# Attention with kept exponentials on one core: the exchange between partition groups goes through a buffer in DRAM, and SyncE's transfers stand in program order

## The chip, the cores and the metric

The kernel runs on one core of a Trainium2 chip (8 cores); the other cores are idle. The metric is the time of one execution on the device in microseconds. A core has TensorE (PE; PEld is its weight load), VectorE (DVE), ScalarE (ACT), GpSimd (POOL) and SyncE (SP, which only issues transfers). POOL, ACT and SP can each put transfers on a queue of their own; the 16 DMA engines of the core work on all of these queues.

## The reference

```python
# x: 8 x 512 x 512, cond: 8 x 512, all float32; 16 heads of 32
Q, K, V   = heads(x @ Wq.T + bq), heads(x @ Wk.T + bk), heads(x @ Wv.T + bv)
tQ, tK    = heads(tokens @ Wq.T + bq), heads(tokens @ Wk.T + bk)   # tokens = cond[:, None, :]
scores    = (Q + tQ) @ (K + tK).T / sqrt(32)
attn      = softmax(scores, axis=-1)
out       = x + (attn @ V, heads joined)
```

## The kernel before, in words

The work is cut into 32 steps `t`, one for each batch and each group of four heads (8 batches of 4 groups). The scores of a step are made twice. First they come row by row (128 queries on the partitions, 512 keys along the free axis): PE makes them (L640), DVE takes the negative row maximum (`nmax`, L592 and L649), and ACT takes the exponentials and their row sums (L700). Of these exponentials half the queries (two blocks of 128) are *kept* for steps 1 to 29 (`KEPT`). For the other half of the queries the scores are made a second time in transposed form (keys on the partitions, L784, after L771 has put the row maxima in), and ACT takes their exponentials (L798). `weighted` (L839) then multiplies exponentials by V, first the half made again, then the kept half; `send` turns the result (L911), scales it (L912), adds the residual `xr` (L913) and stores it (L916).

The kept exponentials have queries on the partitions and must have keys there before L839 can use them. That takes two things. `turn_kept` (L659), four DVE instructions a step, transposes every 32x32 block in place. Then the blocks must change places between the four *partition groups* of 32 partitions: the part at group `a`, place `g` changes with the part at group `g`, place `a`. A part is 32 partitions of 1024 floats, 128 KB; there are six such pairs. `swap_kept(t, move)` does this inside SBUF in three moves: each pair's first part goes aside, the second takes its place, and the part put aside goes to the second's place. That is 18 transfers of 128 KB a step. Some are issued by SP (`nc.sync`) and some by POOL (`nc.gpsimd`): move 2 always by POOL, and of move 0 either none or the last four, so that POOL issues 6 or 10 of them a step.

The loop is `thirds(t, made)` for t = 1 to 28, with three parts `i` = 0, 1, 2. At its start stands `weighted(t - 1)`. Within it the exponentials of step t + 1 are kept and turned, and at its end moves 0 and 1 of step t + 1 are issued; move 2 of step t is issued in part 1. So the parts of step t + 1 set out at the end of `thirds(t)`, and L839 wants them in `thirds(t + 2)`. Beside this work PE makes the projections of the next batch (L461), a third of a set in each part.

The other transfers of a step are SP's: `load_block` (L172) brings an input block `x` in four transfers of 64 KB, `load_residual` (L190) `xr` in four, `send` (L916) stores the output in four, and `turn_max` (L726) is one transposing transfer from `split` to `maxT`, which L771 needs a step later. `split_max` (L714 to L717, on POOL) makes what it reads.

`manual_schedule` names the engines whose instructions stay in the order in which the code is written. Here these are PE, ACT, DVE and POOL; SP is not among them, and the order of its transfers is made by the framework.

Of the kernel before, what the change touches and what calls it, by code (L numbers as in the profile page):

```python
# [9 lines left out]
F32 = mybir.dt.float32  # L10
# [7 lines left out]
def kernel(  # L18
# [38 lines left out]
    nc = tc.nc  # L57
    P = 128
    B, S, D = x.shape
# [3 lines left out]
    HG = P // HD  # L63
# [14 lines left out]
    op = ctx.enter_context(tc.tile_pool(name="op", bufs=2))  # L78
    ring = ctx.enter_context(tc.tile_pool(name="ring", bufs=1, space=bass.MemoryType.PSUM))

    psum = ring.tile([P, 8, 512], F32, tag="psum", name="psum")


# [32 lines left out]
    def banks(i, n=1):  # L116

        row = row_of[0] or [at_end[j] for j in TURNS[turn[0]]]
        j = row[i]
        if n == 1:  # L120
            return psum[:, j, :]
        k = row[i + 1]
        return psum[:, j : k + 1 : k - j, :]
# [103 lines left out]
    def load_w(n, w, queue, cs=range(NC)):  # L227
        wv = w.rearrange("(c p) d -> p c d", p=P)
        for c in cs:
# [7 lines left out]
                mybir.EngineType.Activation,  # L237
                mybir.EngineType.DVE,
                mybir.EngineType.Pool,
            }  # L240
        )
    )
# [415 lines left out]
        e = kept[t][:, :, n // NP, pr, :].rearrange("p g h s -> p g (h s)")  # L658
        nc.vector.transpose(e, e)  # L659

    APART = [(a, g) for a in range(HG) for g in range(a + 1, HG)]
    between = store[:, 16:18]

    def swap_kept(t, move, some=range(6)):

        later = 6 if t % 4 == 1 else 2

        def part(a, g):
            return kept[t][a * BL : (a + 1) * BL, g].rearrange("p c h s -> p (c h s)")

        for n in some:
            a, g = APART[n]
            at = (n + 2) % HG * BL
            aside = (store[:, 6:8] if t == KEPT[-1] else between)[at : at + BL, n // HG]
            aside = aside.rearrange("p i s -> p (i s)")
            to, of = [(aside, part(a, g)), (part(a, g), part(g, a)), (part(g, a), aside)][move]
            if t < KEPT[-1]:
                here = move == 2 or move == 0 and n >= later
            else:
                here = move > 0 and n >= 3  # L680
            (nc.gpsimd if here else nc.sync).dma_start(to, of)  # L681

    def denominators(t, qc, w=HG, js=range(HG)):

        if t >= T - 2:
            return
        keep = t in KEPT and qc < KQ
        if keep and t not in kept:
            kept[t] = room(t)
        for j in js:  # L690
            of = to = banks((w or 0) + j)
            if w is None and j == 0:
                of = to = spare
# [193 lines left out]
    def weighted(t, pt, pd, between):  # L887

        apart = masked(t)
        if t in KEPT:
            of = (0, 2, 1, 3)
            for half in (1, 0):
                for kc in of:
                    times_v_half(t, kc, half, pt, of)
                if half == (t + 1 not in KEPT):
                    spread_sums(apart, pd)
        else:
            for kc in range(NS):  # L900
                times_v(t, kc, pt)
                if kc == (NS - 1 if t + 1 in KEPT else 0):
                    spread_sums(apart, pd)
        rec = reciprocals(t, pd)
        between()
        send(t, pt, rec)
# [195 lines left out]
    turn_kept(1, 3)  # L1102
    combine_x(1, 1, nc.gpsimd)
    aparts[0] = masked(0)
    for move in range(2):
        swap_kept(1, move)

    MADE = [
        (n, u, product)
# [45 lines left out]
    def thirds(t, made):  # L1155

        b, r = divmod(t, G)
        of = (t - 1) // G + 1
        begin(0, HG)
        turn_more(t, 0, 0)  # L1160
        row_max_aside(t + 1, 1)
        max_aside(t + 1, 1)
        row_max(t + 1, 2, False, HG)
        turn_more(t, 0, 1)
        denominators(t + 1, 1, None, (1, 2, 3, 0))
        denominators(t + 1, 2, HG)
        weighted(t - 1, banks(0), banks(1), nothing)
        turn_more(t, 0, 2)
        load_blocks(1)
        one_item(of, *next(made), (2, 3), ignore, nothing)  # L1170
        released(0, 1, 4, 5, 7, 6, 2, 3)
        for i in (1, 2):
            begin(HG)
            rows = (t + 1, 3) if i == 1 else (t + 2, 0)
            if i == 1:
                joined(t, i - 1, rows)
                turn_more(t, i, 0)
                row_max(*rows, False, HG, False)
            else:
                exponentials_of_rest(t, i - 1)  # L1180
                turn_more(t, i, 0)
                row_max(*rows, False, HG)
            turn_more(t, i, 1)
            if i == 1:
                first = range(6 if t + 1 < KEPT[-1] else 3)
                swap_kept(t, 2, first)
                split_max(t + 1)
                turn_max(t + 1)
                swap_kept(t, 2, range(len(first), 6))
            dens = lambda js=range(HG): denominators(*rows, HG, js)  # L1190
            n, u, kind = next(made)
            if kind == "first":
                products(of, n, u, kind, False, dens, nothing, None)
                turn_more(t, i, 2)
            elif n == "v":
                small = nothing
                if t + 1 not in KEPT:
                    small = lambda: transpose_max(t + 1, banks(2), nc.scalar.copy)
                other_shared(of, n, u, dens, (0, 3), small, lambda: turn_more(t, i, 2))
                released(1, 2, 4, 5, 6, 7, 0, 3)  # L1200
            else:
                products(of, n, u, kind, False, dens, nothing, False)
                turn_more(t, i, 2)
            if i == 1:
                aparts[t] = masked(t)
            if (t + 1, i) == (KEPT[-1], 1):
                swap_kept(t + 1, 0)
            if i == 2:
                if r == 0:
                    combine_x(b + 1, 1, nc.gpsimd)  # L1210
                load_residual(t + 1)
            else:
                if t > 1:
                    bias_residual(t)
                if r == 0:
                    combine_x(b + 1, 0, nc.gpsimd)
            if i == 2 and t + 1 < KEPT[-1]:
                for move in range(2):
                    swap_kept(t + 1, move)

    def other_shared(b, n, u, dens, at, small, more):

# [115 lines left out]
        row_max_of(t + 1, 2, 1, banks(HG + 2, 2))  # L1338
    row_max_of(t + 1, 2, 0, late[0][:, :2, :])
    bias_residual(t)  # L1340
    swap_kept(t, 1)
    apart = masked(t - 1)
    aparts[t] = masked(t)
    load_residual(t + 2)
    bias_residual(t + 2)
    swap_kept(t, 2)
    load_residual(t + 1)
    halves_of(t - 1, banks(0), (1,))
    row_of[0] = [*second[:2], *first[2:], *first]
# [150 lines left out]
```

## Time and profile before

| | |
|---|---|
| median of 3 runs | 650.57 us (649.7 to 651.48) |
| the profiled execution | 650.74 us, span of the core 648.9 us |
| PE, DVE, ACT, POOL busy | 642.6, 600.7, 533.6, 409.6 us |
| granted clock of TensorE | 1.0 |
| transfers between places in SBUF | 264 issued by SP, 258 by POOL, 128 KB each |
| queue of SP (q1) | 65.54 MB, packets took 53.3% of 16 engines' span |
| queue of POOL (q0) | 33.83 MB, packets took 19.2% of 16 engines' span |

The time of a run is a little longer than the span, 650.74 against 648.9 us for the same execution. A queue's share is the time that its packets took, added over the 16 DMA engines and divided by 16 spans: 53.3% of 648.9 us are 346 us in which all 16 engines would be busy with that queue.

### The profile page before, as it was taken

The page shows a single profiled execution, that of the slowest core. Times are in us where ns is not written, and L with a number is a line of the kernel's source. Part 1 is how long each engine was busy: PE and PEld are TensorE (multiplying, and loading weights), DVE is VectorE, ACT ScalarE, POOL GpSimd, SP SyncE. Part 2 cuts the span into 40 slices and gives each one's busy share as a digit, 9 for nine tenths or more (in the row PEclk, how much of TensorE's full clock was granted, in tenths as well). Part 3 has the DMA queues.
Part 4 walks back from the last instruction along what each step waited for, and adds up shares of the span by engine and source line. Part 5 has one row for each costly group of instructions (what it writes and reads, how often), then busy time and mean ns, then how long its engine had stood idle before and what let it go on. Part 6 is the DMA issues. An engine that isn't in the chain of part 4 may idle for free. (4 is left out here: it accounts for less than half of the span.)

```text
span 648.9 us, 24878 instructions
## 1 busy us (share of the span) xinstructions
PE 642.6 (99%) x9856; PEld 358.5 (55%) x9856; DVE 600.7 (93%) x845; ACT 533.6 (82%) x1364; POOL 409.6 (63%) x651
## 2 busy tenths in 40 slices
PE   9999999999999999999999999999999999999997
PEld 8445555556555555555555555555655555555541
DVE  3799999999999999999999999999999999999887
ACT  2479888889888889888888988898988888888564
POOL 3642555767666785668566585766767677675650
PEclk9999999999999999999999999999999999999999
DMA  7634588788779788878788887897877777777821
GB/s 187 106 48 68 121 183 175 158 180 178 155 172 181 156 190 181 190 155 172 173 184 172 171 170 152 177 198 158 180 152 180 176 162 153 165 177 161 201 37 33
DMA packets 248456, 102.01 MB, mean 157 GB/s; under 512 B 229962, under 2 KB 230474, under 8 KB 248340
## 3 DMA queue, kind: packets, MB, share of 16 engines
q1 hardware_dynamic: 234196, 65.54, 53.3%
q0 software_dynamic: 12384, 33.83, 19.2%
q8 instruction: 78, 1.28, 0.8%
q10 hardware_dynamic: 1760, 1.05, 0.6%
q14 instruction: 38, 0.31, 0.2%
HBM read 19.75 MB, written 8.39 MB: 43 GB/s over the span
## 5 line engine op out<-in xcount | busy, mean ns | idle before, releaser
L592 DVE TENSOR_REDUCE nmax<-psum 128x1 f32<-128x512 f32 x279 | 177.8, 676 | 9.9 <-PE psum L640 5.1
L681 POOL DMA_DIRECT2D store<-store x258 | 128.9, 502 | 77.3 <-DMA store<-store 51.9
L700 ACT ACTIVATE psum<-psum,nmax 128x512 f32<-128x512 f32 x248 | 165.1, 678 | 3.6 <-DVE nmax L592 3.0
L640 PE MATMUL psum<-kT,qT 32*128 32x512 f32 x1024 | 161.8, 612 | 0.0
L700 ACT ACTIVATE store<-psum,nmax 128x512 f32<-128x512 f32 x204 | 139.5, 700 | 24.7 <-DVE nmax L592 24.5
L798 ACT ACTIVATE store<-psum 128x512 f32<-128x512 f32 x232 | 119.8, 603 | 33.4 <-PE psum L784 33.4
L659 DVE STREAM_TRANSPOSE store<-store 128x1024 f32<-128x1024 f32 x116 | 138.9, 1217 | 0.0
L649 DVE TENSOR_REDUCE nmax<-psum 128x2 f32<-128x1024 f32 x98 | 118.9, 1213 | 0.0
L839 PE MATMUL psum<-store,v 128*32 128x256 f32 x1856 | 107.1, 381 | 0.6 <-issue 0.6
L839 PEld LDWEIGHTS psum<-store,v 128*32 128x32 f32 x1856 | 57.2, 110 | 57.9 <-ACT wT_q L631 21.2
L784 PE MATMUL psum<-qT,kT 32*128 32x256 f32 x928 | 83.8, 373 | 0.0
L640 PEld LDWEIGHTS psum<-kT,qT 32*128 32x128 f32 x1024 | 61.3, 183 | 35.5 <-issue 17.8
L912 POOL TENSOR_TENSOR res<-res,recs 128x512 f32<-128x512 f32 x30 | 31.4, 1045 | 75.4 <-DVE res L911 75.4
L784 PEld LDWEIGHTS psum<-qT,kT 32*128 32x128 f32 x928 | 60.8, 184 | 5.7 <-issue 0.3
L700 ACT ACTIVATION_READ_ACCUMULATOR psum<-psum,nmax 128x1 f32 x248 | 55.1, 222 | 0.0
L461 PE MATMUL psum<-wc_v,xc 128*32 128x256 f32 x768 | 47.7, 379 | 0.0
L203 POOL TENSOR_TENSOR xr<-xr,bvs 128x512 f32<-128x512 f32 x30 | 38.3, 1276 | 11.1 <-DMA x<-in_x_dram 11.1
L461 PE MATMUL psum<-xc,wc_q 128*32 128x256 f32 x720 | 44.8, 379 | 0.0
L461 PE MATMUL psum<-xc,wc_k 128*32 128x256 f32 x720 | 44.5, 379 | 0.0
L700 ACT ACTIVATION_READ_ACCUMULATOR store<-psum,nmax 128x1 f32 x204 | 44.4, 218 | 0.0
L913 POOL TENSOR_TENSOR res<-res,xr 128x512 f32<-128x512 f32 x30 | 38.3, 1276 | 2.4
L461 PE MATMUL psum<-xT,wT_k 128*32 128x256 f32 x480 | 34.5, 382 | 0.0
(191 smaller groups left out, 975.4 us busy)
## 6 DMA issues: line engine op xcount, KB each, us to landing
store<-store SPq DMA_DIRECT2D x264, 128.0 KB, 2.9
store<-store POOLq DMA_DIRECT2D x258, 128.0 KB, 3.8
out_dram<-res SPq DMA_DIRECT2D x122, 64.0 KB, 3.7
xr<-in_x_dram SPq DMA_DIRECT2D x120, 64.0 KB, 3.4
x<-in_x_dram SPq DMA_DIRECT2D x112, 64.0 KB, 3.5
w_q<-in_L_cond_Wq_dram SPq DMA_DIRECT2D x4, 256.0 KB, 4.5
w_v<-in_L_cond_Wv_dram SPq DMA_DIRECT2D x16, 64.0 KB, 2.5
w_k<-in_L_cond_Wk_dram SPq DMA_DIRECT2D x16, 48.0 KB, 2.8
```

Of the source, the lines that this page charges most:

```text
L203: nc.gpsimd.tensor_tensor(xr[t], xr[t], bias, ALU.add)
L461: nc.tensor.matmul(pt[r], still[:, r], moving, start=(kc == kcs[0]), stop=(kc == kcs[-1]))
L592: nc.vector.tensor_reduce(nmax[t][:, qc, j : j + 1, 0], pt, AX.X, ALU.max, negate=True)
L640: nc.tensor.matmul(pt, qkT["q", t][r, qc * P : (qc + 1) * P], qkT["k", t][r, :], start=True, stop=True,)
L649: nc.vector.tensor_reduce(nmax[t][:, qc, pr * 2 : pr * 2 + 2, 0], pt, AX.X, ALU.max, negate=True)
L659: nc.vector.transpose(e, e)
L681: (nc.gpsimd if here else nc.sync).dma_start(to, of)
L700: nc.scalar.activation(to, of, AF.Exp, bias=nmax[t][:, qc, j, :], accum_out=sums[t][:, qc, j, :],)
L784: nc.tensor.matmul(banks(j)[:, i * HS : (i + 1) * HS], qkT["k", t][r, kc * P : (kc + 1) * P], qkT["q", t][r, KQ * P :], start=False, stop= ...
L798: nc.scalar.activation(e[:, j], banks(j), AF.Exp)
L839: nc.tensor.matmul(pt[j * HD : (j + 1) * HD, half * HS : (half + 1) * HS], vs[b % 2][:, kc, (g * HG + j) * HD : (g * HG + j + 1) * HD], e, ...
L913: nc.gpsimd.tensor_tensor(y, y, xr.pop(t), ALU.add)
```

## The change

The six pairs no longer change places inside SBUF. A buffer in DRAM (pool `outside`, two buffers, `outer[t]`) takes all parts that have to move, in six writes of one to three parts each (`write_kept`), and six reads (`read_kept`) bring them back to their new places. Together that is 12 parts written and 12 read. The parts on the diagonal stay where they are. All twelve transfers are issued by SP; POOL issues none.

SP joins the engines with a written order. With this the places of the calls are set by hand: the writes of step t + 1 stand at the end of `thirds(t)`, behind them the loads of `x` and of `xr`; the reads of step t stand in part 0 of `thirds(t)`, ahead of `weighted(t - 1)` and so ahead of its stores. The two chunks of SBUF that were used to put parts aside stay reserved.

```diff
+    outside = ctx.enter_context(
+        tc.tile_pool(name="outside", bufs=2, space=bass.MemoryType.DRAM)
+    )
...
                 mybir.EngineType.Pool,
+                mybir.EngineType.SP,
...
-    APART = [(a, g) for a in range(HG) for g in range(a + 1, HG)]
-    between = store[:, 16:18]
-    def swap_kept(t, move, some=range(6)):
...
-            (nc.gpsimd if here else nc.sync).dma_start(to, of)
+    OTHERS = [(0, 1, 4), (1, 0, 1), (1, 2, 4), (2, 0, 2), (2, 3, 4), (3, 0, 3)]
+    def write_kept(t):
+        outer[t] = outside.tile([HG, BL, HG, NP * 2 * S // 2], F32, tag="kept", name=f"outer_{t}")
+        of = kept[t].rearrange("p g c h s -> p g (c h s)")
+        for a, lo, hi in OTHERS:
+            nc.sync.dma_start(outer[t][a, :, lo:hi], of[a * BL : (a + 1) * BL, lo:hi])
+    def read_kept(t):
+        to = kept[t].rearrange("p g c h s -> p g (c h s)")
+        for g, lo, hi in OTHERS:
+            nc.sync.dma_start(
+                to[g * BL : (g + 1) * BL, lo:hi],
+                outer[t][lo:hi, :, g].rearrange("a j f -> j a f"),
+            )
...
         denominators(t + 1, 2, HG)
+        read_kept(t)
         weighted(t - 1, banks(0), banks(1), nothing)
         turn_more(t, 0, 2)
-        load_blocks(1)
...
-                first = range(6 if t + 1 < KEPT[-1] else 3)
-                swap_kept(t, 2, first)
                 split_max(t + 1)
                 turn_max(t + 1)
-                swap_kept(t, 2, range(len(first), 6))
...
             if (t + 1, i) == (KEPT[-1], 1):
-                swap_kept(t + 1, 0)
+                write_kept(t + 1)
...
-                load_residual(t + 1)
+                if t + 1 == KEPT[-1]:
+                    load_blocks(1)
+                    load_residual(t + 1)
...
             if i == 2 and t + 1 < KEPT[-1]:
-                for move in range(2):
-                    swap_kept(t + 1, move)
+                write_kept(t + 1)
+                load_blocks()
+                load_residual(t + 1)
...
     bias_residual(t)
-    swap_kept(t, 1)
+    read_kept(t)
...
-    swap_kept(t, 2)
     load_residual(t + 1)
```

On SP, in the middle of the loop, one step of the order before runs from one transposing transfer to the next (`out_dram<-res` is the store of an output, `store<-store` a swap):

```order
L726 DMA_TRANSPOSE maxT_2551<-split 128x4x128
L190 DMA xr_2654<-in_x_dram 32x16x32 x2
L172 DMA x_2743<-in_x_dram 32x16x32 x4
L681 DMA store<-store 32x1024 x8
L916 DMA out_dram<-res_2733 32x16x32 x4
L190 DMA xr_2922<-in_x_dram 32x16x32 x3
L726 DMA_TRANSPOSE maxT_2810<-split 128x4x128
```

After the change SP has these twelve rows between one transposing transfer and the next four stores; `outer` is the buffer in DRAM, and 1024, 2048 and 3072 floats a partition are one, two and three parts:

```order
L673 DMA outer_2101<-store 32x3072
L673 DMA outer_2101<-store 32x1024
L673 DMA outer_2101<-store 32x2048 x2
L673 DMA outer_2101<-store 32x1024
L673 DMA outer_2101<-store 32x3072
L175 DMA x_2108<-in_x_dram 32x16x32 x4
L193 DMA xr_2113<-in_x_dram 32x16x32 x4
L679 DMA store<-outer_2101 32x3x1024
L679 DMA store<-outer_2101 32x1024
L679 DMA store<-outer_2101 32x2x1024 x2
L679 DMA store<-outer_2101 32x1024
L679 DMA store<-outer_2101 32x3x1024
```

Eight or twelve swaps of SP have become twelve transfers that carry 24 parts, and the stores and the transposing transfer of the next step stand behind all of them.

On POOL, at the start of a step (L912 and L913 finish an output, L1249 and L1250 belong to the projection of V, L714 begins `split_max`), the order before has:

```order
L532 TENSOR_TENSOR kT_2087<-kT_2087 128x256
L681 DMA store<-store 32x1024 x4
L912 TENSOR_TENSOR res_2203<-res_2203,recs_2201 128x512
L913 TENSOR_TENSOR res_2203<-res_2203,xr_1858 128x512
L1249 TENSOR_TENSOR v_163<-v_163 128x256
L1250 TENSOR_TENSOR v_163<-v_163 128x256
L681 DMA store<-store 32x1024 x6
L714 COPY split<-nmax_2078 128x16
```

and after the change:

```order
L536 TENSOR_TENSOR kT_2064<-kT_2064 128x256
L913 TENSOR_TENSOR res_2186<-res_2186,recs_2184 128x512
L914 TENSOR_TENSOR res_2186<-res_2186,xr_1852 128x512
L1249 TENSOR_TENSOR v_165<-v_165 128x256
L1250 TENSOR_TENSOR v_165<-v_165 128x256
L715 COPY split<-nmax_2055 128x16
```

The ten swaps are gone and nothing else of POOL has moved. On PE, DVE and ACT the instructions stand in the same order before and after.

More of the change, by code (lines that the diff above doesn't have):

```diff
@@ L659, in turn_kept @@
         nc.vector.transpose(e, e)
-    APART = [(a, g) for a in range(HG) for g in range(a + 1, HG)]
-    between = store[:, 16:18]
-    def swap_kept(t, move, some=range(6)):
[L666 to L681, printed above, removed]
+    outer = {}
+    OTHERS = [(0, 1, 4), (1, 0, 1), (1, 2, 4), (2, 0, 2), (2, 3, 4), (3, 0, 3)]
[11 more added lines that the diff above has]
+            )
     def denominators(t, qc, w=HG, js=range(HG)):
@@ L1104 @@
     aparts[0] = masked(0)
-    for move in range(2):
-        swap_kept(1, move)
+    write_kept(1)
     MADE = [
@@ L1217, in thirds @@
             if i == 2 and t + 1 < KEPT[-1]:
-                for move in range(2):
-                    swap_kept(t + 1, move)
+                write_kept(t + 1)
+                load_blocks()
+                load_residual(t + 1)
     def other_shared(b, n, u, dens, at, small, more):
```

## The prediction

> **What bounds the kernel now.** I read the page's busy times first, then the rhythm of the steps in the timeline, then the waits of the loop, and last the DMA queues. A measurement of this kernel can tell about 0.3% (2 us) from no change.
>
> The page's row of busy times:
>
> ```profile
> PE 642.6 (99%) x9856; PEld 358.5 (55%) x9856; DVE 600.7 (93%) x845; ACT 533.6 (82%) x1364; POOL 409.6 (63%) x651
> ```
>
> PE is busy all the time and DVE almost. POOL has room. How long a step is, the timeline of POOL shows at L912, once a step:
>
> ```profile
> 304.06 1.05 POOL L912 TENSOR_TENSOR res<-res,recs 128x512 f32<-128x512 f32 x1 [0.26 <-DVE res L911]
> 323.24 1.04 POOL L912 TENSOR_TENSOR res<-res,recs 128x512 f32<-128x512 f32 x1 [3.22 <-DVE res L911]
> 342.40 1.04 POOL L912 TENSOR_TENSOR res<-res,recs 128x512 f32<-128x512 f32 x1 [3.22 <-DVE res L911]
> ```
>
> A step takes (342.40 - 304.06) / 2 = 19.17 us. Then the waits between 100 and 580 us, 25 steps: first POOL's longest for a transfer, then two ordinary ones of PE ("issue" is a wait for nothing that shows), then every one in which PE or DVE waits for POOL or for a transfer:
>
> ```profile
> POOL store L681 <- DMA store<-store: 49.4, 45, 3.2
> ...
> PEld psum L461 <- ACT store L798: 25.4, 44, 0.8
> ...
> PEld L771 <- issue: 18.5, 45, 0.4
> ...
> PEld L771 <- DMA store<-store: 2.1, 5, 0.4
> ...
> PEld psum L461 <- POOL qT L538: 1.5, 4, 0.4
> ...
> PEld psum L461 <- POOL res L913: 0.4, 1, 0.4
> ...
> DVE qT L554 <- POOL qT L540: 0.2, 1, 0.2
> ```
>
> The exchange costs POOL waiting, and PE and DVE nearly nothing: 2.1 + 1.5 + 0.4 + 0.2 = 4.2 us in 25 steps. So the swaps are hidden now, and little can be won by making them cheaper. What can be lost depends on how full the DMA engines get. The window of the loop and its queues:
>
> ```profile
> 100.00:580.00 480.00, 479.35 (x7812) 273.32 (x7808) 458.92 (x623) 419.61 (x1089) 329.84 (x538) 1.00 0.80 171
> ```
> ```profile
> q1 hardware_dynamic: 174100, 51.26, 56.3%
> q0 software_dynamic: 10817, 29.55, 22.4%
> q8 instruction: 62, 1.02, 0.9%
> q14 instruction: 30, 0.25, 0.2%
> issues: line engine op xcount, KB each, median us to landing
> store<-store POOLq DMA_DIRECT2D x226, 128.0 KB, 3.7
> store<-store SPq DMA_DIRECT2D x224, 128.0 KB, 2.9
> xr<-in_x_dram SPq DMA_DIRECT2D x102, 64.0 KB, 3.8
> out_dram<-res SPq DMA_DIRECT2D x100, 64.0 KB, 4.1
> x<-in_x_dram SPq DMA_DIRECT2D x82, 64.0 KB, 3.8
> maxT<-split SPq DMA_TRANSPOSE x25, 2.7
> ```
>
> The 16 engines are taken for 0.80 of the time, 0.80 x 19.17 = 15.3 us a step. This is the resource the change spends.
>
> **What one transfer takes of the engines.** Two stretches price the small ones. Between 28 and 34 us only loads of `x` and `xr` ran, between 62.5 and 68.5 us only one transposing transfer:
>
> ```profile
> q1 hardware_dynamic: 5059, 0.63, 67.0%
> ```
> ```profile
> q1 hardware_dynamic: 544, 0.13, 11.0%
> ```
>
> 0.67 x 6 us for 0.63 MB, which is 9.6 pieces of 64 KB, makes 0.42 us each; 0.11 x 6 = 0.66 us for the transposing one. In the loop q1 took 0.563 x 480 = 270.2 us. Take away 284 pieces of 64 KB at 0.42 (119.3) and 25 transposing ones (16.5): 134.4 us are left for 224 swaps of SP, 0.60 us a part of 128 KB. POOL's took 0.224 x 480 / 226 = 0.48 us. Both together: 0.54.
>
> **The change part by part.** *POOL's 258 issues go.* POOL is not the bound; the waits above that could go with them are 4.2 us, and I count zero: L538 stands behind L912 and L913, not behind a swap, and the waits of L771 are as long (0.4 us) as those that it has for no releaser. The lower bound is -4.2 us.
>
> *SP's issue time.* SP's rows for a swap and for the transposing transfer (ns, shortest/median/longest):
>
> ```profile
> L681 SPq DMA_DIRECT2D store<-store x264: 507/542/1990, 68.9 to 612.1; - x132
> ```
> ```profile
> L726 SPq DMA_TRANSPOSE maxT<-split x29: 1207/1225/3522, 62.5 to 598.9; - x29
> ```
>
> A step has now 6 writes, 6 reads, 4 loads of `x`, 4 of `xr`, 4 stores and the transposing one. 24 x 0.54 + 1.2 is about 14 us of 19.17. It fits, so I count nothing.
>
> *The order on SP.* The reads wait for the writes; behind them stand the stores and the transposing transfer. Writes can start when the last L659 of a step ends, and the parts must be back when L839 takes the kept half a step later, the second half of its run. These rows are that L659, the issue-to-landing time (2.3 us) of the first twelve swaps of SP, and two runs of L839:
>
> ```profile
> 316.50 1.23 DVE L659 STREAM_TRANSPOSE store<-store 128x1024 f32<-128x1024 f32 x1
> ```
> ```profile
> store<-store SPq DMA_DIRECT2D x12, 128.0 KB, 2.3
> ```
> ```profile
> 317.70 3.66 PE L839 MATMUL psum<-store,v 128*32 128x256 f32 x64
> 336.86 3.44 PE L839 MATMUL psum<-store,v 128*32 128x256 f32 x60
> ```
>
> From 317.7 to 336.9 + 1.7 = 338.6 are 20.9 us. Needed at 0.60 us a part: writes 7.2, eight loads 3.4, reads 7.2, and a landing of 2.3: 20.1 us. It just fits, with 0.8 us to spare. The loads between writes and reads cover the landing of the writes. The transposing transfer has time: L771 needs it a step later.
>
> *The load of the ring.* Before, 18 parts a step; now 12 written and 12 read, 24. All go through SP's queue. The sum of a step is 24 x u + 12 x 0.42 + 0.66 + 0.21 (q8 and q14, 1.1% of 19.17), so 24 u + 5.91. It exceeds 19.17 us where u is over 0.55 us. What is u? The trace has no large transfer between DRAM and 32 partitions. The nearest rows, share and GB/s in the last two columns: SP's first twelve swaps with no other large transfer beside them, one slice of them, the wide loads of the start (128 partitions from DRAM, two queues), and a stretch with swaps of both queues:
>
> ```profile
> 69.90:76.90 7.00, 7.00 (x111) 3.75 (x107) 7.00 (x11) 6.24 (x19) 2.50 (x3) 1.00 0.86 198
> 72.00:73.00 1.00, 1.00 (x28) 0.51 (x24) 1.00 (x2) 1.00 (x5) 0.00 (x0) 1.00 0.91 205
> 4.00:6.00 2.00, 1.88 (x11) 1.68 (x9) 0.00 (x0) 0.53 (x1) 0.00 (x0) 1.00 1.05 402
> 606.00:608.00 2.00, 2.00 (x36) 1.06 (x40) 2.00 (x4) 0.98 (x2) 1.48 (x2) 1.00 0.92 285
> ```
>
> By the wide loads u is 0.131 MB / 402 GB/s = 0.33 us; by SP's swaps alone 0.86 x 7 us for 1.39 MB (10.6 parts) = 0.57; in the loop 0.60; by the slice's plain rate 0.131 / 205 = 0.64. The ends are 0.33 and 0.64. I take 0.60: the new transfers have one side on 32 partitions, as the swaps have, and they have one queue, as SP's swaps have. The Trainium skill, "SBUF — State Buffer", section "Door 1: The DMA port swizzle", speaks against the 402 GB/s row here: 32 partitions reach 8 of 16 ports, about 218 GB/s, by which a part would be an estimated 0.60 us and the time the one forecast here, where the wide row alone would leave it unchanged. The trace agrees so far as SP's swaps never ran faster.
>
> Sum: 24 x 0.60 + 5.91 = 20.31 us, 1.14 more than a step has. Once the ring is the slowest thing there is no gap to make up: stores, the transposing transfer and the next writes are ready when the reads have gone out, so a step takes 20.31 us and PE waits at the kept half of L839. This holds where `x` is still loaded, one block a step. The changed program loads 28 blocks by its order, 6 of them ahead of the loop, so 22 steps; in the other 6 the sum is 20.31 - 1.68 = 18.63 us and fits. 22 x 1.14 = 25 us.
>
> *The end.* The exchange of step 29 must land before the last kept half, at 619.06, and its last L659 ends at 599.00 + 2.36 = 601.4:
>
> ```profile
> 599.00 2.36 DVE L659 STREAM_TRANSPOSE store<-store 128x1024 f32<-128x1024 f32 x2
> ```
> ```profile
> 619.06 1.29 PE L839 MATMUL psum<-store,v 128*32 128x256 f32 x20
> ```
>
> Writes 7.2, four loads of `xr`, reads 7.2 and a landing of 2.3 make 18.4 us, 619.8: up to 0.7 us late, inside the uncertainty of u; I count 0.
>
> From the profiled execution's 650.74 us this is 675.8; it lies 0.17 us over the median of 650.57, so **676 us**.
>
> **The rivals.** *Hidden after all.* The engines keep up because a part takes less than 0.55 us. For it: the stretch at 606 us moved 285 GB/s (0.46 us a part), the larger transfers come in fewer pieces, and the mean over both queues in the loop is 0.54 us. Against it: the fast stretches had two queues. At 0.54 the sum is 18.9 us, under a step, and the time is 650.6. The Trainium skill, "DMA: Bandwidth & Descriptors", section "Issuing engines are not separate DMA queues", says that a second issuing engine saves only issue time; by it this rival would be right in taking 0.54. The trace speaks against it with 0.60 for SP and 0.48 for POOL.
>
> *Faster: POOL is relieved.* The place is L461's weight loads, L771 and L554, which wait for POOL or a swap; the price is their 4.2 us, and it decides only if u is below 0.55 and those waits hang on the 10 swaps in POOL's order. 650.6 - 4.2 = 646.4 us. For it: POOL gives back 226 issues in the loop and 49.4 us of waiting. Against it: each of the waits is at most 0.4 us and none is put to L681's issue.
>
> *Heavier than forecast.* Writing to DRAM and reading from it cost the plain rate of 0.64 us: 24 x 0.64 + 5.91 = 21.27, 2.1 us over for 22 steps, and 0.42 us over for the other six: 46.2 + 2.5 = 49 us, 699 us. For it: SP's swaps alone got no further than 205 GB/s at a share of 0.91. Against it: 0.64 counts the gaps between SP's issues, which larger transfers don't have.
>
> **How the numbers follow.** Chances: forecast 0.48 (u from 0.57 to 0.62: 5.91 + 13.68 = 19.59 gives 22 x 0.42 = 9 us, 660; 20.79 gives 36 us, 686), heavier 0.20, hidden 0.17, faster 0.15. Slower by over 0.3% is 0.48 + 0.20 = 0.68, the same 0.17, faster 0.15. The range must reach from the hidden case to beyond the heavier one: 647 to 708 leaves out most of the faster case and a ring that is still slower, near 0.2 together. For the slower cases alone it would be 660 to 708.
>
> **What would show it.** Right: steps of about 20.3 us at L913 where `x` is loaded and 19.2 us in the last ones; a new wait of PE at the kept half of L839 on a transfer `store<-outer`, about 1 us a step; a DMA share near 1.0 and about 205 GB/s in the loop; the row of PE's waits for ACT smaller, since others come first. Wrong: steps of 19.17 us with a share of 0.9 or less (a part takes under 0.55 us, and the ring isn't the bound); PE waiting at L771 for `maxT` (the order on SP, not the load); or steps under 19.1 us (POOL mattered).

## The result and the profile after

| | before | after |
|---|---|---|
| median in the same comparison | 651.03 us (649.7 to 652.34) | 741.65 us (740.27 to 743.93) |
| span of the profiled execution | 648.9 us | 740.0 us |
| ratio of the times | | 1.140, 95% interval 1.136 to 1.143 |

The change makes the kernel 14.0% slower. The forecast, 676 us with a range up to 708, had the direction and the resource right. The loss is 91 us where 25 were counted. "The ring" below is SP's queue (q1) with the 16 DMA engines behind it, as in the prediction.

The page after: busy time of PE and DVE, the granted clock and the DMA share in forty slices, SP's queue, and the group of L840 (it was L839).

```profile
PE 673.8 (91%) x9856; PEld 377.1 (51%) x9856; DVE 608.9 (82%) x845; ACT 537.9 (73%) x1364; POOL 284.4 (38%) x393
...
PEclk9999998998999999999989999999999999999899
DMA  7534898898989999889989899898999999899951
...
q1 hardware_dynamic: 243796, 122.17, 83.2%
...
L840 PE MATMUL psum<-store,v 128*32 128x256 f32 x1856 | 127.3, 421 | 51.8 <-DMA out_dram<-res 42.0
```

The engines do the same work in a longer span. The DMA slices stand at 8 and 9 through the loop, and PE has a new wait of 51.8 us at L840, which multiplies by V. The waits from 100 to 680 us show the same (us in total, times, longest):

```profile
DVE recs L885 <- PE psum L875: 47.5, 17, 5.2
PE psum L840 <- DMA out_dram<-res: 42.0, 18, 4.1
...
```

PE waits at the kept half for the exchange, and DVE then waits for PE. The releaser shown is a store of the output, which L840 doesn't read; what it reads are the parts. They are read back by the transfers just ahead of those stores on SP. With part of the reads moved (run split_reads, below) the same wait is put to `store<-outer`.

Where the 91 us lie is read from the starts of L913 (L912 before), one a step. After, then before:

```profile
92.93 1.05 POOL L913 TENSOR_TENSOR res<-res,recs 128x512 f32<-128x512 f32 x1 [5.84 <-DVE res L912]
...
548.98 1.05 POOL L913 TENSOR_TENSOR res<-res,recs 128x512 f32<-128x512 f32 x1 [10.29 <-DVE res L912]
...
673.50 1.05 POOL L913 TENSOR_TENSOR res<-res,recs 128x512 f32<-128x512 f32 x1 [5.85 <-DVE res L912]
...
707.69 1.05 POOL L913 TENSOR_TENSOR res<-res,recs 128x512 f32<-128x512 f32 x1 [3.42 <-DVE res L912]
```
```profile
93.41 1.04 POOL L912 TENSOR_TENSOR res<-res,recs 128x512 f32<-128x512 f32 x1 [3.21 <-DVE res L911]
...
592.23 1.04 POOL L912 TENSOR_TENSOR res<-res,recs 128x512 f32<-128x512 f32 x1 [3.22 <-DVE res L911]
...
618.64 1.04 POOL L912 TENSOR_TENSOR res<-res,recs 128x512 f32<-128x512 f32 x1 [4.37 <-DVE res L911]
```

The first 20 steps, in which `x` is still loaded, take (548.98 - 92.93) / 20 = 22.80 us, the next six (673.50 - 548.98) / 6 = 20.75 us. Before, all 26 take (592.23 - 93.41) / 26 = 19.19 us. That is 20 x 3.61 = 72 us and 6 x 1.56 = 9 us. The next output comes after 34.2 us where it came after 26.4: 8 us. The remaining 2 us lie behind it. (The forecast counted 22 steps with `x`; the first of them lose nothing, since the output at 92.93 us came at 93.41 us before.)

**What a part costs.** The transfers from 100 to 600 us: share of SP's queue, then issues, KB each and median us to landing.

```profile
q1 hardware_dynamic: 167298, 89.70, 90.2%
...
store<-outer SPq DMA_DIRECT2D x45, 384.0 KB, 6.2
outer<-store SPq DMA_DIRECT2D x44, 384.0 KB, 4.4
store<-outer SPq DMA_DIRECT2D x46, 256.0 KB, 6.5
outer<-store SPq DMA_DIRECT2D x44, 256.0 KB, 4.5
store<-outer SPq DMA_DIRECT2D x45, 128.0 KB, 6.1
xr<-in_x_dram SPq DMA_DIRECT2D x89, 64.0 KB, 2.6
out_dram<-res SPq DMA_DIRECT2D x88, 64.0 KB, 7.0
outer<-store SPq DMA_DIRECT2D x44, 128.0 KB, 3.8
x<-in_x_dram SPq DMA_DIRECT2D x84, 64.0 KB, 3.4
maxT<-split SPq DMA_TRANSPOSE x22, 5.5
```

These are 536 parts of 128 KB. By the prediction's working, 451.0 us less 261 x 0.42 and 22 x 0.66 leaves 326.9 us, 0.61 us a part. The forecast said 0.60. So the work asked of the ring was foreseen, but the ring stands still for part of each step: its share in this window is 0.91 at 182 GB/s, which leaves 0.09 x 22.8 = 2.1 us of a step with `x` idle. The Trainium skill, "SBUF — State Buffer", section "Door 1: The DMA port swizzle", gives about 218 GB/s for 32 partitions, by estimate 0.60 us a part; the trace agrees with 0.61.

**Where the ring is idle.** First SP's own timeline for one step (start, duration), then a table by stage. In the table DMA share and GB/s are the last two columns, the clock stands ahead of them; in a short stretch the share can come out a little over 1.

```profile
318.12 5.51 SPq L673 DMA_DIRECT2D outer<-store  x6
323.68 4.06 SPq L175 DMA_DIRECT2D x<-in_x_dram  x4
327.79 2.08 SPq L193 DMA_DIRECT2D xr<-in_x_dram  x4
329.91 2.83 SPq L679 DMA_DIRECT2D store<-outer  x6
332.85 2.61 SPq L917 DMA_DIRECT2D out_dram<-res  x4
336.21 4.62 SPq L727 DMA_TRANSPOSE maxT<-split  x1
340.94 5.40 SPq L673 DMA_DIRECT2D outer<-store  x6
```
```profile
318.00:323.00 5.00, 4.74 (x92) 3.29 (x96) 2.62 (x4) 1.22 (x4) 1.54 (x2) 1.00 0.93 187
323.00:326.00 3.00, 3.00 (x52) 2.09 (x48) 2.32 (x4) 2.12 (x5) 2.20 (x3) 1.00 0.95 262
326.00:332.00 6.00, 6.00 (x104) 3.28 (x100) 5.52 (x8) 5.62 (x16) 1.42 (x6) 1.00 0.65 108
332.00:340.00 8.00, 5.62 (x84) 2.43 (x76) 7.79 (x12) 6.76 (x20) 7.30 (x6) 1.00 1.07 216
340.00:341.00 1.00, 0.33 (x4) 0.23 (x8) 0.40 (x1) 1.00 (x3) 0.00 (x0) 0.54 0.34 58
```

The rows take 5.51 + 4.06 + 2.08 + 2.83 + 2.61 + 4.62 = 21.7 of the 22.8 us of this step. They hold some waits between issues; the single issues add up to 19.9 us. That alone is no loss: before the change SP's issues filled 362 of the 449 us from 100 to 549 us, with PE busy all the time. While the writes and the reads run, the ring's share is 0.93 to 1.07. In the six microseconds from 326, when the writes drain and the loads of `x` and `xr` follow, it is 0.65 at 108 GB/s: 2.1 us idle. Behind the transposing transfer, which holds SP for 4.62 us, one microsecond has a share of 0.34: 0.7 us idle. These two gaps make most of what the sum left out: a step with `x` takes 22.80 - 20.31 = 2.5 us more than counted.

### The profile page after: what moved, and what is told of

It is laid out like the page before. It is cut to its first block, busy times and chain, and to the rows that moved or that the text cites. A ratio compares the mean times of both kernels' runs of the same rounds, so it can differ in the third digit from the quotient of the medians.

```text
span 740.0 us, 24102 instructions
## 1 busy us (share of the span) xinstructions
PE 673.8 (91%) x9856; PEld 377.1 (51%) x9856; DVE 608.9 (82%) x845; ACT 537.9 (73%) x1364; POOL 284.4 (38%) x393
## 5 line engine op out<-in xcount | busy, mean ns | idle before, releaser
L840 PE MATMUL psum<-store,v 128*32 128x256 f32 x1856 | 127.3, 421 | 51.8 <-DMA out_dram<-res 42.0
L644 PE MATMUL psum<-kT,qT 32*128 32x512 f32 x1024 | 164.6, 618 | 0.0
L840 PEld LDWEIGHTS psum<-store,v 128*32 128x32 f32 x1856 | 63.6, 118 | 119.1 <-DMA out_dram<-res 34.0
L913 POOL TENSOR_TENSOR res<-res,recs 128x512 f32<-128x512 f32 x30 | 31.5, 1049 | 197.7 <-DVE res L912 197.7
L785 PE MATMUL psum<-qT,kT 32*128 32x256 f32 x928 | 85.9, 383 | 0.0
L885 DVE RECIPROCAL recs<-psum 128x16 f32<-128x16 f32 x28 | 7.1, 255 | 50.1 <-PE psum L875 47.5
L465 PE MATMUL psum<-wT_v,xT 128*32 128x256 f32 x512 | 37.7, 410 | 0.0
```

Source lines behind the costliest of these rows:

```text
L465: nc.tensor.matmul(pt[r], still[:, r], moving, start=(kc == kcs[0]), stop=(kc == kcs[-1]))
L644: nc.tensor.matmul(pt, qkT["q", t][r, qc * P : (qc + 1) * P], qkT["k", t][r, :], start=True, stop=True,)
L785: nc.tensor.matmul(banks(j)[:, i * HS : (i + 1) * HS], qkT["k", t][r, kc * P : (kc + 1) * P], qkT["q", t][r, KQ * P :], start=False, stop= ...
L840: nc.tensor.matmul(pt[j * HD : (j + 1) * HD, half * HS : (half + 1) * HS], vs[b % 2][:, kc, (g * HG + j) * HD : (g * HG + j + 1) * HD], e, ...
L913: nc.gpsimd.tensor_tensor(y, y, rec.broadcast_to([P, NB, BL]), ALU.mult)
```

## The experiments

The theory to be tested is that one queue is too slow for the step's transfers because it is loaded to the limit and also stands idle between them; against it stand the written order on SP, the number of transfers as such, the wait of the reads for the writes, and PE's clock. Times are medians; the kernel before took 649.6 to 651.5 us beside them. Ratios are to the kernel before.

### Is it the bytes?

**half_bytes**: all twelve transfers in the same places, half of each part.

```diff
-  nc.sync.dma_start(outer[t][a, :, lo:hi], of[a * BL : (a + 1) * BL, lo:hi])
+  nc.sync.dma_start(outer[t][a, :, lo:hi, :512], of[a * BL : (a + 1) * BL, lo:hi, :512])
   ... (reads alike)
```

> The kernel after with the same 12 transfers in the same order on SP, but only the first half of each part (512 of 1024 floats) is written and read; the rest of the kept parts stays unexchanged. Theory A (bytes: a part takes 0.6 us of the 16 engines and a step has more work than time): a step needs 24 x 0.30 + 5.9 = 13 us, the exchange is hidden again, 648 to 656 us. Theory B (the written order and the number of transfers on SP, each waiting for the one eight before it): the same 25 issues with the same waits, still over 710 us.

Measured 650.27 us, ratio 1.000 (0.999 to 1.001): the whole loss is gone. The stages from 100 to 580 us as one row, then SP from its writes to its reads:

```profile
100.00:580.00 480.00, 480.00 (x7816) 272.96 (x7816) 459.19 (x623) 420.56 (x1090) 220.13 (x313) 1.00 0.61 130
```
```profile
312.51 2.75 SPq L673 DMA_DIRECT2D outer<-store  x6
315.37 2.10 SPq L175 DMA_DIRECT2D x<-in_x_dram  x4
317.51 3.32 SPq L193 DMA_DIRECT2D xr<-in_x_dram  x4
320.87 2.83 SPq L679 DMA_DIRECT2D store<-outer  x6
```

With the ring at 0.61, PE is busy all the time. An issue here takes 2.75 / 6 = 0.46 us for a write and 2.10 / 4 = 0.53 us for a load. With whole parts the six writes took 5.51 us, so a loaded ring makes SP wait.

**seven_eighths**: `:896` in the same places, just under the limit of the prediction's formula.

> The same twelve transfers a step, each with 896 of the 1024 floats of a part (the last eighth of each part does not change places, so the output is not the reference's). By the prediction's own formula, without gaps, a step asks 24 x 0.613 x 7/8 + 5.91 = 18.8 us of the ring, under TensorE's 19.17: 650 to 656 us. With the two microseconds of idle ring per step that the trace after shows, it asks about 20.9 us: 680 to 705 us.

Measured 688.22 us, ratio 1.059 (1.056 to 1.061). The formula without gaps, 18.8 us a step, is refuted; with 2 us of idle ring it holds.

**order_only**: the kernel before, with SP put under the written order and nothing else changed.

```diff
                 mybir.EngineType.Pool,
+                mybir.EngineType.SP,
```

> The kernel before, with the swaps inside SBUF, and SP added to the engines whose order is the written one; nothing else. Theory A (bytes): 648 to 655 us, the bytes are those of before. Theory B (order on SP): a good part of the loss of 91 us, over 680 us.

Measured 659.56 us, ratio 1.014 (1.004 to 1.023): more than theory A allowed and far less than B. There are two runs, 657.28 and 661.84 us, so the size, some 9 us with the swaps, is uncertain; half_bytes has a written order too and loses nothing, so it is no fixed price.

### What are the gaps worth?

**no_turn**: the transposing transfer is left out from step 2 on; all later steps use the row maxima of step 1.

```diff
+        if t > 1:
+            maxT[t] = maxT[1]
+            return
         maxT[t] = op.tile([P, S], BF16, tag="maxT", name=f"maxT_{t}")
```

> The kernel after, where the transposing transfer of maxT is made once, for step 1, and the steps 2 to 29 use that one: 28 transposing transfers are left out. Theory C (behind the reads the transposing transfer holds SP for 3.8 us and the ring runs dry before the next writes, some 1 us beside its own 0.66 us): 28 x 1.7 = 47 us less, about 695 us. Theory A alone (only its 0.66 us of the engines): 28 x 0.66 = 18 us less, about 723 us.

Measured 697.13 us, ratio 1.071 (1.067 to 1.076). It saves 44.5 us, 1.6 us for each of 28, where 0.66 was counted: theory C.

**loads_pool**: POOL issues the loads of `x` and `xr` in the loop.

```diff
-                nc.sync.dma_start(xs[n][h * BL : (h + 1) * BL], spread(x[b], cc * P + h * BL))
+                (nc.gpsimd if n >= 10 else nc.sync).dma_start(
+                    xs[n][h * BL : (h + 1) * BL], spread(x[b], cc * P + h * BL)
+                )
   ... (xr alike, for 1 < t < 28)
```

> The kernel after with the loads of x and xr in the loop issued by POOL; SP has the writes, reads, stores and the transposing transfer. Theory F (between writes and reads SP's eight loads run the 16 engines at a share of 0.6 only, some 2 us of each step): reads can follow the writes at once, 690 to 715 us. If the loads are only moved and the engines are full anyway: 735 to 745 us. If POOL is held up by its own loads as it was by the reads: over 750 us.

Measured 691.12 us, ratio 1.064 (1.062 to 1.067): 50.5 us saved by eight small transfers a step that are still made, but not issued by SP. The time is in theory F's range, but the trace doesn't show F's mechanism. SP's longest wait from 100 to 580 us, and POOL's queue from 100 to 640 us:

```profile
SPq L681 <- DMA outer<-store: 86.8, 32, 5.6
```
```profile
q0 software_dynamic: 5888, 12.07, 10.4%
```

The reads don't follow the writes at once; with no loads between them SP now waits for the writes to land. The ring's share is 0.92, and a step with `x` takes 20.49 us (the first 20, by the rhythm of the outputs), so 1.6 us a step are still idle where 2.1 were. Of the 2.3 us that a step gains some 0.4 are idle time; the rest is packet time: a load on POOL's queue takes 0.104 x 540 / 184 = 0.31 us of the engines, not 0.42. So this run shows that the eight loads are dear on SP's queue, not that idle time makes them so.

**loads_noturn**: both edits.

> Both of the edits that helped one at a time: the loads of x and xr in the loop are issued by POOL, and the transposing transfers of all steps but the first are left out, so the exponentials of the later steps use the row maxima of step 1 and the output is not the reference's. The loads alone saved 50 us, the transposing transfers alone 45 us. Theory L (two separate losses of the ring on SP's queue, the stretch of small loads and the stretch behind the transposing transfer): they add, until TensorE's 19.2 us a step is the bound again: 650 to 665 us. Theory M (both take away the same idle time of the ring, whatever gives it): little beyond the better of the two, 680 to 692 us.

Measured 666.25 us, ratio 1.024 (1.022 to 1.027), just over theory L's upper end and 14 us below theory M. The loads and the transposing transfer are largely two separate losses: together they give 75 us, where the two savings add up to 95 and no more than 91 can be won. Of the last 16 us, 9.5 lie in the loop of the profiled execution (26 steps take 508.3 us, before 498.8; about one step in four is 2 to 3 us longer) and the rest behind it; what makes them was not tested.

### Why are the loads so dear?

**read_previous**: reads take the parts written one step earlier, so they don't wait for the writes just ahead; a third buffer keeps them.

```diff
-                outer[t][lo:hi, :, g].rearrange("a j f -> j a f"),
+                outer[max(t - 1, 1)][lo:hi, :, g].rearrange("a j f -> j a f"),
```

> The reads of a step take the parts that were written one step earlier (a third buffer in DRAM keeps them), so no read waits for the writes just ahead of it; number, size and order of all transfers stay. The exchanged exponentials are then those of the step before and the output is not the reference's. Theory N (the ring idles around the loads because the reads behind them wait until the last write has landed): 2 us a step go, 685 to 705 us. Theory K (it idles there because eight small loads can't fill it): 735 to 745 us.

Measured 742.65 us, ratio 1.141 (1.138 to 1.144). In this order the wait of the reads for the writes costs nothing; theory N falls. With the loads taken out from between them the wait is there (loads_pool).

**loads_rows** (eight loads of 64 KB to 32 partitions, 2 KB pieces), **loads_one** (two loads of 256 KB to 128 partitions) and **loads_wide** (eight loads of 64 KB to 128 partitions, 512-byte pieces). The three calls for `xr` in the loop, with their helpers written out and shortened; `x` alike:

```diff
 loads_rows
+    xr[t][h * BL : (h + 1) * BL], x[b][g * P + h * BL : ...].rearrange("j (f e) -> j f e", e=BL)
 loads_one
+    xr[t], x[b][g * P : (g + 1) * P].rearrange("j (f e) -> j f e", e=BL)
 loads_wide
+    xr[t][:, h * 4 : h * 4 + 4], x[b][g * P : (g + 1) * P, h * P : ...].rearrange(...)
```

> The loads of x and xr in the loop stay on SP, eight of 64 KB in the same places, but each reads 32 whole rows of x, 2 KB a partition in one piece, where it took pieces of 128 bytes; so the loads bring other elements and the output is not the reference's. Theory P (the ring is slow in the stretch of the loads because of their small pieces, and SP spends its time on writing them out): the stretch shrinks to what 512 KB cost at the parts' rate or less, about 2.4 us, and the time falls by 1 to 3 us a step with x, to 680 to 720 us. Theory Q (eight further transfers each with its own wait and issue, whatever their pieces): 732 to 745 us.

> As the run with whole rows, and x and xr in the loop come in one transfer of 256 KB over all 128 partitions each: two loads a step where there were eight. The output is not the reference's. Theory P: within 10 us of the run with eight loads of whole rows. Theory Q: this run alone falls, to 690 to 715 us. If both hold, the two runs fall one after the other.

> The loads of x and xr in the loop are again eight transfers of 64 KB in the same places on SP, but each goes to all 128 partitions (512 bytes to each) where a load of whole rows goes to 32 (2 KB to each); other elements are brought and the output is not the reference's. Eight loads of whole rows took 725.8 us, two transfers over all partitions 685.1 us: they differ in number and in the partitions. If the number is what counts (SP's issue and the wait of each), this run stays at 720 to 735 us. If a transfer to 32 partitions is what is slow, it falls to 683 to 700 us.

Measured 725.83 (ratio 1.113, 1.109 to 1.118), 685.06 (1.051, 1.047 to 1.055) and 729.55 us (1.122, 1.116 to 1.127). Larger pieces save 16 us. Eight loads cost nearly the same to 32 or to 128 partitions; two in place of eight save 41 us more. So it is the number of SP's issues. The shares agree: 0.88 from 100 to 600 us in loads_rows, 0.87 in loads_wide, 0.93 in loads_one. SP in loads_one, one step:

```profile
331.56 5.26 SPq L683 DMA_DIRECT2D outer<-store  x6
336.87 0.43 SPq L179 DMA_DIRECT2D x<-in_x_dram  x1
337.35 1.91 SPq L200 DMA_DIRECT2D xr<-in_x_dram  x1
```

The loads take SP 2.3 us here and 6.1 us in the kernel after. An issue of about half a microsecond feeds the ring 64 KB, which it moves in 0.42 us; the same issue feeds it a read of 128 to 384 KB, 0.6 to 1.8 us of work. Eight small ones in a row let the ring run empty. By these figures alone eight issues of 0.49 us leave only 8 x 0.07 = 0.6 us idle; what else slows that stretch, small pieces among it, was not separated. A second limit goes by number too: in the program each of SP's transfers also waits for the one issued eight places earlier. In the kernel after, SP's waits show it from 100 to 680 us at the stores (L917 for `store<-outer`, 36.6 us) and at the transposing transfer (20.5 us), but list none at the loads, so it is not what empties the ring there.

**writes_pool**: POOL issues the six writes instead.

```diff
-            nc.sync.dma_start(outer[t][a, :, lo:hi], ...)
+            nc.gpsimd.dma_start(outer[t][a, :, lo:hi], ...)
```

> The kernel after with the six writes of a step issued by POOL instead of SP. POOL is free behind the last transpose of a step, so that here, unlike with the reads, nothing of POOL's is queued behind a long wait. Theory D (two queues overlap and a part takes about 0.50 us): a step needs about 18 us, 655 to 690 us. Theory E (the ports of 32 partitions set 0.60 us a part whoever issues): the steps stay over 20 us, 700 to 740 us, the gain only from SP's shorter order.

Measured 711.58 us, ratio 1.094 (1.089 to 1.099): SP relieved of six large issues helps less than of eight small ones, and the time lies where theory E had it: a second queue doesn't bring the exchange under a step.

### Why is the transposing transfer so dear?

**turn_plain**: a plain transfer of the same 128 KB in its place.

```diff
-        nc.sync.dma_start_transpose(maxT[t]..., split[t % 2]...)
+        nc.sync.dma_start(maxT[t], split[t % 2].rearrange("p c h e -> p (c h e)"))   # t > 1
```

> The transposing transfers of all steps but the first become plain transfers of the same 128 KB from the same tile to the same tile, in the same place on SP and with the same waits; row maxima are then not turned and the output is not the reference's. If it is the transposition that costs (its issue and its work on the ring), the time falls to that without these transfers, 697 us, give or take 8. If it is the place of a transfer that waits behind a full ring and holds the writes behind it, 730 to 745 us.

Measured 720.11 us, ratio 1.104 (1.100 to 1.108), between the two theories. Of the 44.5 us, 21.5 go with the transposition and 23 with the plain transfer in its place.

**split_reads**: three of the reads stand behind the transposing transfer.

```diff
-        read_kept(t)
+        read_kept(t, range(3))
...
                 turn_max(t + 1)
+                read_kept(t, range(3, 6))
```

> The computation is whole. Three of the six reads of a step are moved behind the transposing transfer, ahead of the writes of the next step; so fewer parts are queued in front of the transposing transfer. Theory J (it is costly because it waits in a full ring and SP's later transfers wait for it): its issue falls from about 4 us towards 1.2 us, the time to 700 to 720 us. If the transposing transfer costs the ring the same wherever it stands (what its own move of data takes), 735 to 745 us; and over 750 us if the kept half now waits for the later reads.

Measured 729.61 us, ratio 1.122 (1.120 to 1.124): 12 us saved, less than theory J said. The transposing transfer's issue (minimum, median, maximum in ns), after and in this run:

```profile
L727 SPq DMA_TRANSPOSE maxT<-split x29: 1300/3825/4677, 62.1 to 686.4; - x29
```
```profile
L727 SPq DMA_TRANSPOSE maxT<-split x29: 1190/2756/3848, 62.0 to 674.7; - x29
```

With fewer parts ahead of it the median falls from 3.8 to 2.8 us; before the change it was 1.2. The price moves with what is queued, and half the step's reads now come later.

### Moving an issue to another engine can be worse

**reads_pool** (POOL issues the six reads, `nc.gpsimd` in `read_kept`) and **turn_act** (ACT issues the transposing transfer, a little later in the same part of the step):

```diff
 reads_pool
-            nc.sync.dma_start(
+            nc.gpsimd.dma_start(
                 to[g * BL : (g + 1) * BL, lo:hi], ...
 turn_act
-                turn_max(t + 1)
...
             if i == 1:
+                turn_max(t + 1, nc.scalar)
                 aparts[t] = masked(t)
```

> The kernel after with the six reads of a step issued by POOL instead of SP; writes and all else as they were. Theory D (one queue keeps the parts of one partition group, and so half of the ports, in front; two queues overlap, as POOL's and SP's swaps did at 0.48 and 285 GB/s): a step needs about 24 x 0.50 + 5.9 = 18 us, 655 to 690 us. Theory E (who issues does not matter, the 16 engines are the same): 730 to 745 us.

> The kernel after with the transposing transfer of maxT issued by ACT (28 of the 29), behind its exponentials in part 1 of a step, instead of by SP; all bytes and transfers remain. Theory C (it is SP's wait that costs: the transposing transfer waits in SP's order for the reads and the next writes wait behind it): most of the 44 us that leaving it out saved come back, 695 to 715 us. Theory A alone (its own work on the 16 engines costs): 730 to 745 us. ACT's issue time of 1.2 us or more a step lies in gaps of ACT, which is not the bound.

Measured 817.13 us (1.256, 1.248 to 1.263) and 826.69 us (1.269, 1.256 to 1.281). Both are worse than either theory. POOL's waits in reads_pool:

```profile
POOL store L679 <- DMA outer<-store: 65.4, 8, 10.8
POOL store L679 <- DVE nmax L596: 57.5, 6, 9.6
POOL store L679 <- DMA x<-in_x_dram: 47.7, 6, 10.4
```

POOL keeps its written order and stands at the reads until the writes have landed; its own work for PE is behind them. In turn_act: SP's largest wait, then one load of `xr` and the transposing transfer, then the stage between.

```profile
SPq L193 <- DMA maxT<-split: 112.3, 20, 6.9
```
```profile
313.27 7.13 SPq L193 DMA_DIRECT2D xr<-in_x_dram  x4
317.10 1.21 ACTq L727 DMA_TRANSPOSE maxT<-split  x1
```
```profile
316.00:318.00 2.00, 2.00 (x42) 1.19 (x32) 1.83 (x4) 1.93 (x6) 1.06 (x5) 1.00 0.00 0
```

The transposing transfer itself is short (1.21 us), but it waits for ACT's earlier work, and SP's loads wait for it: in the program SP and ACT share the eight counters, and a load of `xr` gets the transfer eight places earlier as its predecessor. The ring is empty for two microseconds.

### The clock

**warm**: 48 small matmuls keep PE busy while it waits for the kept half.

```diff
+                if half == 1 and t + 1 in KEPT:
+                    for _ in range(48):
+                        nc.tensor.matmul(pd[:, 256:384], onesb, onesb, start=True, stop=True)
```

> The kernel after with 48 small bf16 products (128x128, into an unused part of a bank) put on PE in each step between the half made again and the kept half of L840, where PE waits for the reads; nothing else. Theory G (the granted clock falls to 0.5 for some us after a wait of PE of about 4 us, and that costs time): the clock stays near 1.0 and the time falls by 10 to 25 us, 715 to 730 us. Theory A (the 16 DMA engines set the step, and PE's slow stretch lies in its slack): 738 to 748 us, whatever the clock.

Measured 748.97 us, ratio 1.153 (1.151 to 1.155), with a mean clock of 0.995 over the span: 7 us slower than the kernel after. The result is what theory A said, but the run decides less than that. The 48 products take PE 2.85 us a step, with which PE needs 19.2 + 2.85, about 22.1 us. The six steps without `x` take 22.28 us where they took 20.75, with PE busy 133.1 of 134 us: here the products themselves are the bound. Steps with `x` take 22.68 us where they took 22.80, so there the full clock gained 0.1 us, where PE's new load would have allowed some 0.7. In steps with `x` the clock is not what sets the time; for the other steps the run doesn't show it.

## Why the prediction failed, step by step

- **SP's issues: the step that failed first.** "24 x 0.54 + 1.2 is about 14 us of 19.17. It fits, so I count nothing." The 14 us are right for a lightly loaded ring. In a full one SP is held (5.51 us for six writes, 4.62 us for the transposing transfer), and its issues take 19.9 of the 22.8 us of a step. What the sum of issue times could not show is the order: eight issues in a row carry so little that the ring runs down, and SP reaches the reads only behind them.
- **"Once the ring is the slowest thing there is no gap to make up": refuted.** A step with `x` takes 22.80 us where 20.31 was counted, and with a share of 0.91 the ring idles 2.1 us of it, most of that in the stretch of the eight loads. seven_eighths fits only with such gaps, and two loads in place of eight (loads_one against loads_rows) win 41 us.
- **The transposing transfer: mis-sized.** 0.66 us was its work on an idle ring; leaving it out saves 1.6 us a step, since on the crowded queue it also holds SP.
- **Steps without `x`** were said to fit at 18.63 us. They take 20.75: 9 us. Their share is 0.93 from 549 to 673 us, so about 1.5 us of each are idle, with four loads in the stretch where the others have eight.
- **The end** was counted at nothing; it costs 10 us. The sum there was for the last exchange, but what PE waits for is the transposing transfer:

```profile
692.33 0.61 PE L772 MATMUL psum<-maxT,onesb 3*128 3x512 bf16 x4 [2.84 <-DMA maxT<-split]
```

  Behind this wait the clock is 0.50 from 692 to 698 us with PE busy 5.67 of the 6 us, about 2.8 us of work at full clock lost, and a wait of 1.56 us for DVE follows; together they are near the 8 us. The kept parts are back in time: L840 at 710.06 us waits 0.23 us, and for ACT.
- **The cost of a part: right.** 0.60 us forecast, 0.61 measured, on DRAM as within SBUF.
- **The chain from write to read: no limit**, as forecast. read_previous takes its wait away and gains nothing.
- **The rivals.** Hidden (650.6) and faster (646.4) are out, as is the ring at 0.64 us a part: a loaded queue without the gaps would by that rival's own sum have given 699 us. No rival had the gaps as its mechanism; the heavier one was argued down with "gaps between SP's issues, which larger transfers don't have", but eight of the transfers between the writes and the reads stayed small. The Trainium skill, "DMA: Bandwidth & Descriptors", section "Issuing engines are not separate DMA queues", says that other issuing engines save only issue time, "which is usually small relative to the DMA itself". The second half fails here, with 0.49 us of issue (median of `xr`) for 0.42 us of transfer. The first half isn't borne out either: loads_pool saves 50 us, and by its shares most of that is packet time.
- **The signs named beforehand.** Longer steps and the wait of PE at the kept half came. The share near 1.0 at 205 GB/s did not, nor did the 19.2 us of the last steps; 0.91 and 182 GB/s in the loop was the sign that the sum was not the whole. The sign named for the order on SP, PE waiting for `maxT`, came at the end, with 2.84 us.

No kernel run here is faster than the one before; the best with the whole computation and the exchange through DRAM is loads_pool, 691 us.

## What to carry to other kernels

When a queue fed by one engine in program order is the bound, the sum of its work is not enough. Compare, transfer by transfer, the work that an issue carries with the time that the issue takes (here 0.42 us for 0.49, against 0.6 to 1.8 us for a read), and look for the stretches of small transfers and for special transfers behind a full ring. Transfer work that filled 98% of a step by its sum (seven_eighths) did not fit but cost 38 us. Here two loads of the same size together, in larger pieces and with other elements of `x`, did slightly more (685 us) than giving the eight to another engine (691 us), and moving other transfers to POOL or ACT brought waits of its own (817 and 827 us).

## What the hardware showed beyond that

- A transposing transfer holds SP for 1.2 us on a lightly loaded queue and 3.8 us (median) behind six reads and four stores. In its place a plain transfer of the same size costs the kernel about half as much (23 of 44.5 us).
- Behind a wait PE can come back at half clock. In the kernel after, from 341 to 346 us, behind a wait of 3.06 us:

```profile
341.00:346.00 5.00, 5.00 (x80) 2.87 (x76) 1.83 (x3) 1.06 (x5) 0.83 (x1) 0.75 0.94 192
```

The granted clock is 0.75 in the mean of these 5 us (0.50 at first, then 1.00), though PE is busy all the time. The length of the wait doesn't decide alone: behind the wait shown here the clock falls, but behind a longer one the same trace has full clock from 318 to 323 us (the table above):

```profile
318.26 1.93 PE L840 MATMUL psum<-store,v 128*32 128x256 f32 x32 [4.00 <-DMA out_dram<-res]
```

A wait of 2.30 us, at 499.61 us, is followed by half clock. The Trainium skill, "TensorE: Matmul & The Clock Gate", section "What's actually happening", has a half clock after an idle window of about 3.4 us; the trace agrees only roughly, with 2.30 us enough in one place and 4.00 us not in another.
